# Six of a period's graph products ahead of its first transposes, two in each later slot

## The chip, the core and the metric

The kernel runs on one core of a Trainium2 chip. A core has five engines that work through their own instruction queues and wait for each other on semaphores: PE (TensorE, matrix products; its weight loads are shown apart as PEld), DVE (VectorE), ACT (ScalarE), POOL (GpSimd) and SP (SyncE, which here only starts transfers). The metric is the device time of one execution in microseconds (us), lower is better. Before the change nine runs gave a median of 1305.96 us (1296.56 to 1310.61).

## The reference

Two layers of a graph network over N = 2708 nodes with D = 256 features. Layer 0 multiplies a sparse adjacency by x, projects, applies ReLU, and a layer norm of the sum with x. Layer 1, in which the change lies, is this:

```python
R = S + jnp.eye(N, dtype=X.dtype)
R = R / R.sum(-1, keepdims=True)
...
for n in range(STEPS):
    A = _top_p_attention(Xa, W1, W2, W3)
    Xf = R @ Xf
    Xa = A @ Xa
    Z = Z + Xf @ U1[n].T + Xa @ U2[n].T
h = X + Z
...
return (h - mu) / jnp.sqrt(var + LN_EPS) * ln_g + ln_b
```

STEPS is 2, and a last layer norm of the sum with the layer's input follows. `_top_p_attention` makes N x N probabilities (softmax of q k^T), keeps in each row the largest until their sum reaches 0.9, sets the rest to zero and divides by what is left. R is the sparse graph matrix with its rows divided by their sums.

## The kernel before

Rows are cut into NB = 22 blocks of 128 (the last has 20). Everything is fp32. The order on each engine is the order in which the program calls the instructions (a manual schedule); waits come from the data and from the number of buffers of each tile.

Step 1 of the attention runs in a first loop. Its second step, about 775 us to the end, is a loop over *periods* (`per`, L1336), each of six *slots* (`g`, L1350). It is a pipeline over blocks. In period p:

- PE and ACT make the logits and exponentials of block p+2. The logits come in three parts (L535, tile lg, one buffer of two PSUM banks): part 1 is called in slot 1, part 2 in slot 3, and part 0 of the next block in slot 5. ACT takes the exponentials (`exps2`): two of part 0 in slot 0 (L885, L889), one of part 1 in slot 1, one of part 2 in slot 3 (L885). A part of the logits can only be written when the exponentials of the part before it have been read.
- ACT tries two threshold levels for block p+1 (`try_act`, L1027 and L1030, four passes over 2708 columns in slots 0 to 3, 2.64 us each).
- DVE has a generator of steps (`vector_slots`, L1171): it finishes the levels of block p (L1064 to L1074), masks what is above a level (L1084, slot 1), takes candidates (L1091), and for block p-1 sorts them, finds the threshold, marks ties (L1144, slots 4 and 5) and writes the masked probabilities (L1149, end of slot 5, called *the mask* below).
- PE multiplies the masked block p-2 with ya (`turn` and `products`): in slot g four 128 x 128 transposes into a PSUM tile tr (L562, two buffers), a copy by ACT to wT (L564), and two slots later the four products (L591).

The transposes of slot 0 in a period need the mask that DVE wrote last in the period before.

Into this loop the products with R are put (`r_units`, L775, products at L788). R is stored as a compacted list: for each of the 22 row blocks, CC = 7 chunks of 128 gathered columns and one chunk for its own diagonal block, so 8 products of 128 x 128 by 128 x 256 per row block. There are two passes over the 22 blocks: s = 0 multiplies yf and adds v (results go to v_d), s = 1 multiplies v. `units` (L1316) says how many products a period gets: 12 in period 0, 20 in period 1, 16 (two row blocks) in each of periods 2 to 9 (which end pass 0), none in period 10, 16 in each of periods 11 to 21 (pass 1). What a unit carries with it:

- the first unit of a row block m calls the loads for block m+2: the stored chunks (L755, 448 KB), the diagonal block (L756) and the own rows (L772), all started by SP, and puts seven gathers on a list;
- each unit takes one gather off that list (`y_rows`, L745): an indirect transfer of 128 rows of yf or v into one of three buffers, issued by POOL;
- the last unit of a block loads a base (L800 in pass 0, L811 in pass 1) and puts `r_out` two slots ahead, where DVE scales and adds the sum (L817 or L833, tile misc, two PSUM banks).

Blocks whose two sums have both arrived go into the final norm (`final_slot`, L1282): POOL does two multiply-adds for each of up to two blocks (L1265, L1266, called in slot 0, after ACT's normalisation L1250 of the same slot), DVE takes statistics of the result in slot 4 (L1240, L1241), and the next period's slot 0 normalises and stores them. This begins on POOL with period 13.

The even spread that the change replaces is this:

```python
n = n_r * (g + 1) // NG - n_r * g // NG
```

With n_r = 16 and NG = 6 the slots get 2, 3, 3, 2, 3, 3 products. In slot 0 `r_units(n)` stands ahead of `turn`, in the other slots after it (and ahead of the logits of slot 1).

Of the kernel before, what the change touches and what calls it, by code (L numbers as in the profile page):

```python
# [39 lines left out]
ML = 16  # L40
CW, CC = 128, 7
EARLY = 12
AT = 96


# [17 lines left out]
def gnn_two_layer_kernel(ctx: ExitStack, tc: tile.TileContext, N, xT_d, x_d, adj_d, w0_d, b0_d,  # L63
# [30 lines left out]
    assert SEG * (NS - 1) + 8 <= N <= SEG * NS == SEG2 * NS2 and N >= SEG2 * (NS2 - 1) + 8  # L94
    assert SEG * NS - P == (NB - 1) * P - AT and AT + N - (NB - 1) * P <= P
    assert NB == 3 * KS + 1 and CW == P and CAP % 8 == 0 and N < NB * P
# [63 lines left out]
def fast_path(ctx, tc, c, flags, fint, xT_d, x_d, w0_d, b0_d, w1_d, w2_d, w3_d, u1_d, u2_d, g_d, b_d):  # L160
# [19 lines left out]
    def ps_acc(t=None):  # L180
        acc = ps.tile([P, CH], FP, tag="acc", name="acc")
        if t == NB - 1:
            nc.vector.memset(acc[:, :D + 1], 0.0)
        return acc
# [129 lines left out]
    class Lists:  # L314
# [11 lines left out]
        def turn(self):  # L326
            n = self.n
            parts = names[:, self.a:self.b, :].rearrange("p m (s j) -> p (m s) j", j=3)
            tr = ps_tr()
            for j in range(3):  # L330
                nc.tensor.transpose(tr[:n, j, :], parts[:, :, j], ident)
            nc.scalar.copy(self.row[:n].rearrange("q (j p) -> q j p", j=3), tr[:n, :3, :])
# [136 lines left out]
    lists = Lists(0, ML, flags[:, NF - 4:NF - 2], first_room)  # L469
    order = list(range(EARLY)) + [EDGE] + list(range(EARLY, EDGE))  # L470
    for m, prev, then in zip(order, [None] + order, order[1:] + [None]):
# [37 lines left out]
        if ML <= m < EDGE:  # L509
            i, n = m - ML, EDGE - ML  # L510
# [35 lines left out]
    NG = (NB + 3) // 4  # L546
# [34 lines left out]
    def products(keep):  # L581

        if len(before) > keep:
            p, ks, wT, y, acc = before.pop(0)
            for k in ks:
                if p < P:
                    o = EW * (k % 4)
                    nc.tensor.matmul(acc[o:o + p, :D], lhsT=wT[:, k % 4, :p], rhs=part_y(y, k),
                                     start=k < 4, stop=k >= NB - 4)
                    continue  # L590
                nc.tensor.matmul(acc[:p, :D], lhsT=wT[:, k % 4, :p], rhs=part_y(y, k),  # L591
                                 start=k == 0, stop=k == NB - 1)
# [96 lines left out]
    def ya_pair():  # L689
# [15 lines left out]
        p = rows(t0 + 1)  # L705
        nc.scalar.copy(ya[AT:AT + p, t0 + 1, :], pz[:p, 1, :])

# [67 lines left out]
    def r_units(n):  # L775
        for _ in range(n):
            s, m = r_queue[0]
            p = rows(m)
            if not r_now:
                r_now[:] = [ps_misc() if s or m else ps_acc(), 0]  # L780
                if m + 2 < NB:
                    r_load(s, m + 2, True)
            if to_gather:
                y_rows(*to_gather.pop(0))
            acc, k = r_now
            a, y, own = r_in[s, m]
            kw = CW if k < CC else p
            nc.tensor.matmul(acc[:p, :D], lhsT=a[:kw, k, :p], rhs=y[:kw, k, :] if k < CC else own[:p],  # L788
                             start=k == 0, stop=k == CC)
            r_now[1] += 1  # L790
            if k == CC:
                r_now.clear()
                r_queue.pop(0)
                r_in.pop((s, m))
                base = za_load(m) if s else v_load(m)
                later[1].append(lambda s=s, m=m, acc=acc, base=base: r_out(s, m, acc, base))
# [52 lines left out]
    def e2(t):  # L849
        return ring[t % 5]  # L850
# [30 lines left out]
    def shift(b, lg):  # L881
        nc.vector.tensor_reduce(b.nmax, lg[:, :P], AX.X, ALU.max, negate=True)
# [8 lines left out]
    def begin_search(b):  # L891

        nc.vector.tensor_reduce(b.z, b.all[:b.p, :NL], AX.X, ALU.add)
        yield
        nc.vector.reciprocal(b.rz, b.z)
        nc.vector.tensor_scalar(b.nz, b.z, -1.0, None, op0=ALU.mult)
        yield
        nc.vector.tensor_scalar(b.l0, b.roots, b.roots, b.rz, op0=ALU.mult, op1=ALU.mult)
# [44 lines left out]
    for t in range(NB):  # L943
# [6 lines left out]
        if t == 0:  # L950
            nc.vector.memset(x1_edge, 0.0)
            nc.vector.tensor_copy(x1_edge[AT:AT + rows(EDGE)], x1[:rows(EDGE), EDGE, :])
        for g in range(NG):
# [62 lines left out]
    def fifth():  # L1016
        nonlocal scr
        tile2 = big.tile([P, 2 * NW], FP, tag="V", name="e4")
        ring.append(tile2[:, :NW])
        scr = tile2[:, NW:]  # L1020
# [150 lines left out]
    def vector_slots(a, b, begin):  # L1171


        if b and b.t == 0:
            run_all(in_order(b))
            yield
            run_all(threshold(b))
            yield
            for i in range(WS):
                mark(b, i)  # L1180
            yield
            mask(b)
            yield
            run_all(last_level(a))
            below_level(a)
            yield
            run_all(candidates(a))
            run_all(begin)
            yield
            return  # L1190
        order = in_order(b) if b else None
        levels = last_level(a) if a else None
        cands = candidates(a) if a else None
        limits = threshold(b) if b else None
        run_all(turns((part_of_it(order, 7) if b else None, 1), (levels, 1)))
        yield
        if a:
            below_level(a)
        yield
        run_all(turns((order, 1), (part_of_it(cands, 8) if a else None, 2)))  # L1200
        if a and not b:
            run_all(part_of_it(cands, 8))
        yield
        run_all(turns((limits, 1), (cands, 2)))
        yield
        if b:
            mark(b, 0)
            mark(b, 1)
        yield
        if b:  # L1210
            mark(b, 2)
            mark(b, 3)
            mask(b)
        if begin:
            run_all(begin)
        yield
# [119 lines left out]
    for per in range(NB + 2):  # L1336
        if per == 1:
            fifth()
        if per == NB + 1:
            tail.append(True)  # L1340
        n_r = units.get(per, 0)
        b_act = blocks.get(per + 1)
        t_mul = per - 2 if per > 1 else None
        if t_mul is not None:
            accs[t_mul] = ps_acc(t_mul)
        b_exp = None
        if per and per + 2 < NB:
            b_exp = blocks[per + 2] = Block(per + 2)
        vector = vector_slots(blocks.get(per), blocks.get(per - 1), begin_search(b_exp) if b_exp else None)
        for g in range(NG):  # L1350
            n = n_r * (g + 1) // NG - n_r * g // NG
            now = later.pop(0)
            later.append([])
            if g == 0:
                if b_exp:
                    shift(b_exp, lg[0])
                r_units(n)
            if t_mul == EDGE:
                if g == 0:
                    products(0)  # L1360
                    products(0)
                    edge_product(ya, accs[EDGE], e2(EDGE))
            elif t_mul is not None:
                turn(t_mul, g, ya, accs[t_mul], e2(t_mul))
            if b_exp and g == 3:
                lg = logits(1, b_exp.t, 2)
            if g == NG - 1 and 3 < per + 3 < NB:
                lg = logits(1, per + 3, 0)
            if g:
                r_units(n)  # L1370
            if b_exp and g == 1:
                lg = logits(1, b_exp.t, 1)
            if t_mul is not None and t_mul != EDGE:
                products(2)
            if b_exp and g in (0, 1, 3):
                exps2(b_exp, (g + 1) // 2, *lg)
            if b_act:
                for k, part in {0: ((0, 0),), 1: ((0, 1), (0, 2), (0, 3)), 2: ((1, 0),), 3: ((1, 1), (1, 2), (1, 3))}.get(g, ()):
                    try_act(b_act, k, part)
            if per == 0:  # L1380
                ya_pair()
            next(vector)
            if per == 2 and g == 1:
                nc.gpsimd.memset(ring[4][:, N:], 0.0)
            if g == 0:
                final_slot(0)
                if t_mul:
                    t = t_mul - 1
                    base = za_load(t)
                    later[1].append(lambda t=t, base=base: arrive(t, base, accs.pop(t), ras.pop(t)[:rows(t)]))  # L1390
            for f in now:
                f()
            if g and (per < NB + 1 or g < NG - 1):
                final_slot(g)
# [25 lines left out]
    n = len(new) + len(finals)  # L1420
# [384 lines left out]
```

## Time and profile before

| | us |
|---|---|
| median of nine runs | 1305.96 |
| profiled execution, its own time | 1310.5 |
| its span, first to last instruction | 1308.7 |
| PE busy | 1211.5 (93% of the span) |
| DVE busy | 976.0 |
| ACT busy | 733.4 |
| POOL busy | 633.9 |
| mean granted clock of PE | 0.967 |

A row of the timeline gives the start, the duration, the engine, the line, the operation, out<-in tiles, shapes and how many instructions were merged; in brackets how long the engine was idle before it and what released it. An fp32 product shows as two matmul instructions, a transpose as one. PE's ends are modelled, and some records are missing from the trace (around 1040 to 1047 us, for example). A row of the groups ends with the idle time ahead of the group and its main releaser. Periods are told apart by the masks: the one that ends at 909.72 us is the last of period 6, and the products of period 7 begin on PE at 913.47.

### The profile page before, as it was taken

Reading aid. Unit: us, or ns where it says so; the run is one execution under the profiler, and the core shown is the slowest. Engines: PE = TensorE matmul, PEld = TensorE weight load, DVE = VectorE, ACT = ScalarE, POOL = GpSimd, SP = SyncE. Lnnn points to the kernel's source line nnn. Section 1 sums busy time; section 2 is a strip of 40 time slices with the busy share of each in tenths; the row PEclk is TensorE's granted clock in tenths of the full one; section 3 lists DMA queues with packets and bytes.
Section 4 is the critical chain, followed back from the end, with each engine's and each line's share of the span. In section 5 each row is a group of like instructions: output and inputs, shape, how many; then the busy total and the mean of one; then the engine's idle time right before and its main releaser. Section 6 shows DMA issues by size and latency. Waiting matters only on the chain.

```text
span 1308.7 us, 18668 instructions
## 1 busy us (share of the span) xinstructions
PE 1211.5 (93%) x5772; PEld 915.9 (70%) x5772; DVE 976.0 (75%) x3254; ACT 733.4 (56%) x1299; POOL 633.9 (48%) x596
## 2 busy tenths in 40 slices
PE   8999999998899999989996988989998898999885
PEld 6888878843666777767774566767776676777764
DVE  2455564976998888868750387878999878998886
ACT  2010011045555566556562487878989788999822
POOL 1000000014735434777656377767706857888860
PEclk9999999999899999999998898999999998999898
DMA  7465544424122210232233355555525444565441
GB/s 193 163 190 167 170 145 151 160 96 137 47 91 69 71 39 12 89 95 90 84 72 104 119 172 163 176 173 166 169 52 167 150 133 153 164 191 155 146 117 38
DMA packets 104248, 164.92 MB, mean 126 GB/s; under 512 B 20162, under 2 KB 76870, under 8 KB 104138
## 3 DMA queue, kind: packets, MB, share of 16 engines
q1 hardware_dynamic: 77852, 107.57, 25.4%
q0 software_dynamic: 20544, 51.17, 14.1%
q10 hardware_dynamic: 5742, 4.89, 1.3%
q8 instruction: 48, 0.79, 0.3%
q14 instruction: 62, 0.51, 0.1%
HBM read 129.66 MB, written 33.90 MB: 125 GB/s over the span
## 4 chain that ended last, share of the span: by engine, by line
PE 74%; ACT 9%; DVE 8%; issue 3%; POOL 2%; another core or an unknown queue 2%; DMA 1%; ACTq 0%; POOLq 0%; DVEq 0%
PE acc L591 26%; PE acc L274 12%; PE lg L535 9%; PE misc L788 9%; PE tr L562 7%; PE acc L678 2%; PE misc L410 2%; ACT e L1030 2%; PE acc L699 2%; ACT wT L564 2%; PE misc L449 1%; PE misc L727 1%; POOL yg L745 1%; ACT e L885 1%
## 5 line engine op out<-in xcount | busy, mean ns | idle before, releaser
L564 ACT COPY wT<-tr 128x512 f32<-128x512 f32 (+2 forms) x258 | 136.3, 536 | 242.1 <-PE tr L562 153.0
L591 PE MATMUL acc<-x,wT 128*128 128x256 f32 x882 | 224.8, 396 | 17.3 <-ACT wT L564 17.2
L745 POOL DMA_INDIRECT yg<-v_d,ix x154 | 197.6, 1283 | 81.0 <-issue 36.1
L591 PE MATMUL acc<-ya,wT 128*128 128x256 f32 x924 | 229.6, 390 | 4.7 <-issue 4.7
L745 POOL DMA_INDIRECT yg<-yf_d,ix x154 | 183.1, 1189 | 83.9 <-issue 38.9
L591 PEld LDWEIGHTS acc<-x,wT 128*128 128x128 f32 x882 | 163.0, 194 | 79.8 <-ACT wT L564 31.1
L591 PEld LDWEIGHTS acc<-ya,wT 128*128 128x128 f32 x924 | 175.4, 194 | 45.1 <-issue 22.6
L274 PE MATMUL acc<-y,adj_t 128*128 128x257 f32 x924 | 204.4, 379 | 0.0
L274 PEld LDWEIGHTS acc<-y,adj_t 128*128 128x128 f32 x924 | 173.7, 189 | 26.8 <-issue 1.9
L384 POOL DMA_INDIRECT adj_t<-in_adj,ix x154 | 167.3, 1087 | 51.7 <-issue 43.0
L535 PE MATMUL lg<-k,q 64*128 64x512 f32 (+3 forms) x528 | 140.6, 608 | 32.4 <-ACT e L889 14.8
L788 PE MATMUL misc<-yg,adj_t 128*128 128x256 f32 (+1 forms) x602 | 160.4, 395 | 2.0 <-issue 1.1
L562 PE MATMUL tr<-ident,e 128*128 128x128 f32 (+1 forms) x946 | 148.8, 277 | 14.1 <-DVE e L1149 8.4
L562 PEld LDWEIGHTS tr<-ident,e 128*128 128x128 f32 (+1 forms) x946 | 120.8, 145 | 51.1 <-issue 19.1
L788 PEld LDWEIGHTS misc<-yg,adj_t 128*128 128x128 f32 (+1 forms) x602 | 107.1, 192 | 41.6 <-issue 21.2
L351 POOL DMA_DIRECT2D part_d<-e x1 | 0.6, 576 | 272.5 <-DVE e L350 272.5
L1027 ACT ACTIVATE e<-e,st 128x2708 f32<-128x2708 f32 (+1 forms) x43 | 113.6, 2641 | 0.0
L1030 ACT ACTIVATE e<-e,st 128x2708 f32<-128x2708 f32 (+1 forms) x42 | 110.9, 2641 | 0.0
L462 ACT COPY x1T<-tr 128x256 f32<-128x256 f32 (+1 forms) x22 | 8.0, 364 | 174.6 <-PE tr L461 174.6
L597 DVE MAX8 cand<-e 128x8 f32<-128x170 f32 (+1 forms) x352 | 86.8, 319 | 24.1 <-ACT e L542 18.1
L1091 DVE MAX8 cand<-w 128x8 f32<-128x170 f32 (+1 forms) x352 | 94.1, 321 | 0.1
L535 PEld LDWEIGHTS lg<-k,q 64*128 64x128 f32 (+1 forms) x528 | 40.0, 185 | 65.3 <-issue 23.5
(254 smaller groups left out, 1795.4 us busy)
## 6 DMA issues: line engine op xcount, KB each, us to landing
adj_t<-in_adj SPq DMA_DIRECT2D x42, 704.0 KB
adj_t<-adjc_d SPq DMA_DIRECT2D x44, 448.0 KB
adjc_d<-adj_t SPq DMA_DIRECT2D x22, 256.0 KB
base<-za_d SPq DMA_DIRECT2D x40, 128.0 KB
adjc_d<-adj_t SPq DMA_DIRECT2D x22, 192.0 KB
xt<-in_x ACTq DMA_DIRECT2D x21, 128.0 KB
x_d<-x SPq DMA_DIRECT2D x21, 128.0 KB
x1b_d<-xb SPq DMA_DIRECT2D x21, 128.0 KB
```

The lines of the kernel that those rows point to most:

```text
L274: nc.tensor.matmul(acc[:p, :n], lhsT=halves[k // KH][:, k % KH, :p], rhs=y[:, k, :n], start=k == 0, stop=stop and k == NB - 1)
L384: nc.gpsimd.indirect_dma_start(out=a[:CW, i, :], out_offset=None, in_=adj_rows, in_offset=bass.IndirectOffsetOnAxis(ap=ix[:CW, m, i:i + 1] ...
L535: nc.tensor.matmul(lg[:p, h, at:at + b - a], lhsT=q[o, t * P:t * P + p], rhs=keys[s][o, i, :b - a], start=True, stop=True)
L562: nc.tensor.transpose(tr[:, k % 4, :p], columns(e[:p], k), ident[:p, :p])
L564: nc.scalar.copy(wT[:, :len(ks), :p], tr[:, :len(ks), :p])
L591: nc.tensor.matmul(acc[:p, :D], lhsT=wT[:, k % 4, :p], rhs=part_y(y, k), start=k == 0, stop=k == NB - 1)
L597: nc.vector.max(dst[:p, i * 8:(i + 1) * 8], src[:p, i * step:i * step + w])
L745: nc.gpsimd.indirect_dma_start(out=yg[:CW, m % 3, i, :], out_offset=None, in_=rows_d, in_offset=bass.IndirectOffsetOnAxis(ap=ix[:CW, m, i: ...
L788: nc.tensor.matmul(acc[:p, :D], lhsT=a[:kw, k, :p], rhs=y[:kw, k, :] if k < CC else own[:p], start=k == 0, stop=k == CC)
L1027: nc.scalar.activation(scr[:b.p, :N], e, AF.Relu, bias=b.nz, scale=b.l[k], accum_out=b.relu)
L1030: nc.scalar.activation(scr[:b.p, :N], e, AF.Sign, bias=b.nz, scale=b.l[k], accum_out=b.sign)
L1091: nc.vector.max(b.cand[:p, 8 * i:8 * i + 8], low[:p, SEG2 * i:SEG2 * (i + 1)])
```

## The change

In periods after the first that have products, slot 0 gets six of them and each later slot an equal share of the rest:

```diff
@@ -40,6 +40,7 @@
 ML = 16
 CW, CC = 128, 7
 EARLY = 12
+HEAD = 6
 AT = 96
 
 
@@ -1349,6 +1350,9 @@
         vector = vector_slots(blocks.get(per), blocks.get(per - 1), begin_search(b_exp) if b_exp else None)
         for g in range(NG):
             n = n_r * (g + 1) // NG - n_r * g // NG
+            if per > 1 and n_r:
+                ahead = min(n_r, HEAD)
+                n = (n_r - ahead) * g // (NG - 1) - (n_r - ahead) * (g - 1) // (NG - 1) if g else ahead
             now = later.pop(0)
             later.append([])
             if g == 0:
```

With 16 products the slots get 6, 2, 2, 2, 2, 2. The number of instructions on every engine stays. With the products move their gathers on POOL (six ahead of a period's multiply-adds instead of two), the loads of a period's second row block (from slot 3 to slot 2), and the first row block's base load (slot 2 to 1) and `r_out` (slot 4 to 3, on DVE ahead of the marks).

## The prediction

> **What bounds the kernel now.** The change touches step 2 alone, so I read the page's totals and costliest groups first, then a table of stretches, then the timeline inside single periods.
>
> ```profile
> PE 1211.5 (93%) x5772; PEld 915.9 (70%) x5772; DVE 976.0 (75%) x3254; ACT 733.4 (56%) x1299; POOL 633.9 (48%) x596
> ...
> L535 PE MATMUL lg<-k,q 64*128 64x512 f32 (+3 forms) x528 | 140.6, 608 | 32.4 <-ACT e L889 14.8
> L788 PE MATMUL misc<-yg,adj_t 128*128 128x256 f32 (+1 forms) x602 | 160.4, 395 | 2.0 <-issue 1.1
> ...
> L562 PE MATMUL tr<-ident,e 128*128 128x128 f32 (+1 forms) x946 | 148.8, 277 | 14.1 <-DVE e L1149 8.4
> ```
>
> The last row is what the change addresses: in the whole program the transposes waited 8.4 us for the mask. The table of stretches (us; busy PE, PEld, DVE, ACT, POOL; clock) says where PE has idle time to fill:
>
> ```profile
> 891.20:958.00 66.80, 66.80 (x331) 52.30 (x330) 58.69 (x195) 59.55 (x96) 44.69 (x37) 1.00 0.57 167
> 1105.70:1175.30 69.60, 67.74 (x331) 52.09 (x331) 67.03 (x222) 65.95 (x111) 58.57 (x49) 1.00 0.56 173
> 1175.30:1246.80 71.50, 65.46 (x316) 52.35 (x315) 61.46 (x225) 62.99 (x108) 59.27 (x53) 0.95 0.49 152
> ```
>
> Each row is three periods. In the first (periods 6 to 8) PE is never idle: 22.3 us a period. In the second (15 to 17) a period takes 23.2, in the third (18 to 20) 23.8. One slot 0 and 1 of the first kind, period 7, in the timeline:
>
> ```profile
> 914.34 0.60 PE L562 MATMUL tr<-ident,e 128*128 128x128 f32 x4
> ...
> 914.97 0.59 ACT L564 COPY wT<-tr 128x512 f32<-128x512 f32 x1 [2.16 <-PE misc L788]
> ...
> 916.88 1.11 ACT L889 ACTIVATE e<-lg,st 128x1024 f32<-128x1024 f32 x1
> ...
> 916.94 1.46 PE L788 MATMUL misc<-yg,adj_t 128*128 128x256 f32 x6
> ...
> 918.33 1.13 PE L535 MATMUL lg<-k,q 64*128 64x512 f32 x4
> ```
>
> ACT sat idle 2.16 us until the transposes came, copied them, did two exponentials, and only then the slot's logits could overwrite lg. From transposes to logits it is 3.99 us here, and the same in periods 6 (892.05 to 896.05), 8 (936.62 to 940.61) and 9 (958.90 to 962.89): ACT's chain sets it, and PE's own work fills it to within 0.1. Late in the step the releaser is another:
>
> ```profile
> 1191.86 0.75 POOL L1265 TENSOR_TENSOR u<-u,gb 128x256 f32<-128x256 f32 x1
> 1192.68 0.72 POOL L1266 TENSOR_TENSOR u<-u,x1b 128x256 f32<-128x256 f32 x1
> ...
> 1193.44 0.43 DVE L1240 BATCH_NORM_STATS2 bst<-u 128x6 f32<-128x256 f32 x1 [2.14 <-issue]
> ...
> 1194.93 0.43 DVE L1240 BATCH_NORM_STATS2 bst<-u 128x6 f32<-128x256 f32 x1 [0.85 <-POOL u L1266]
> ...
> 1197.26 3.05 DVE L1149 SCALAR_TENSOR_TENSOR e<-w,st,e 128x2720 f32<-128x2720 f32 x1
> 1197.59 3.54 POOL L745 DMA_INDIRECT yg<-v_d,ix  x1 [0.30 <-issue]
> ...
> 1200.47 0.63 PE L562 MATMUL tr<-ident,e 128*128 128x128 f32 x4 [1.03 <-DVE e L1149]
> ```
>
> POOL's multiply-add ends, DVE's statistics start at once, then the marks, the mask, and the transposes. POOL itself runs without a break from 1089.3 to 1268.3: its groups of multiply-adds start at 1166.20, 1191.86 and 1217.52, 25.7 apart, which is 12 gathers of 0.95+0.30, two that run beside a wide DVE operation (3.54+0.30), and four operations of 0.73 to 0.75 with their spaces. So from period 18 on the mask is late because POOL is full, and PE's wait is only the end of that.
>
> **The change part by part.** No instruction is added or removed on any queue. In 19 periods (2 to 9 and 11 to 21) four of sixteen products move to the front: slots 1 to 5 lose 1, 1, 0, 1, 1.
>
> *Products on PE.* Three products take 1.30 (from 928.23 to the next group at 929.53), so one is 0.43 and four are 1.73. In a PE-bound period the first transposes come 1.73 later, and ACT, which waits for them, with them. Between transposes and slot 1's logits there are now two products instead of three, so PE gets there 0.43 earlier while ACT still needs 3.99: 0.43 of new idle time. Everything else of the 1.73 is work done earlier. Periods 2 to 9: 8 x 0.43 = 3.5. Period 11 had 0.44 of waiting ahead of its transposes which the products now fill: 0. Periods 12 and 13: 0.9. Together +4.3. Bounds: 0, if ACT's start does not follow the transposes, and +13 (second rival).
>
> *The first transposes of period 14.* They start at 1077.54, when the two products end and 0.16 after the mask (1077.38). Four products later they delay ACT's normalisation (L1250), for which POOL's second group waited: 2.27 us, until 1089.33. From that point POOL has no gap, so what is late there stays: +1.7. Bounds 0 and 1.73.
>
> *Gathers on POOL.* Six of a period's gathers instead of two now stand ahead of its multiply-adds: four times 1.25 = 5.0, or 7.6 if one falls under a wide DVE operation. This is paid once, not per period, since 14 gathers still lie between two groups; in periods 2 to 9 there are no multiply-adds and POOL has time (44.7 busy of 66.8). In this execution POOL waited 8.75 and 2.27 for ACT before its first two groups, so the gathers lie in that idle time: 0. Without it the groups come with the gathers' own start (3.5 later) plus 5.0 = 8.5 in place of the 4.3 + 1.7 = 6.0 above.
>
> *Tail.* After period 20's group 8 gathers are left instead of 12, so period 21's comes 5.0 earlier. DVE's wait of 0.84 on it and PE's 0.70 and 0.99 on the last gathers go. Next late is the mask, since DVE is busy 21.0 of that period's 22.35: -0.8. Bounds 0 and -3.4 (PE's waits and its four products, too).
>
> *What costs nothing.* Moved with the products: SP's three loads for the second product (0.32 to 0.43 each, slot 3 to 2; they are needed a period later), the base load (slot 2 to 1, used two slots on as before), and the first product's r_out, 0.48 of DVE, from slot 4 to 3, ahead of the marks. A new meeting: the second product needs the bank that the previous r_out frees in slot 1. In period 7 that ends at 917.71 and PE would come at 922.0; in period 19 (1207.08 against 1206.9) it is 0.2, where PE has idle time anyway. DVE's waits for the previous block's sum in slot 2 (11.0 us in seven waits) grow by up to 1.7; the mask in period 7 was ready 4.6 before its transposes, in 15 to 17 between 3.6 and 1.5, and the transposes move 1.7 too. Were this cover gone, each would cost up to 1.7.
>
> In periods 15 to 17 the same chain on ACT (23.2 busy of 24.2) reaches to slot 5's logits, three products leave it, and a period grows by up to 1.3, to 24.5. That stays under POOL's 25.7, and the 2.14+0.85 that DVE waits in each of periods 18 to 20 absorb it: 0.
>
> Nor do the products shorten the 3.65 and 3.71 us before the masks of periods 20 and 21. They come out of the same period's end, and PE reaches the wait earlier by as much.
>
> Sum: 4.3 + 1.7 - 0.8 = +5.2, or 8.5 - 0.8 = +7.7 where POOL has no idle time to lend. Its 11.0 us are more than 5.0, but the profiled execution took 1310.5 (span 1308.7), 4.5 above the median 1305.96, and idle time of that kind is a likely part of the 4.5. I take +6.0, nearer the first: 1316.5 for the profiled execution, **1312.0** for the median.
>
> *A rule beside the rows.* Around 1084.5 to 1092.0, after the 3.58 us wait for logits at 1081.6, the granted clock was 0.54; it was 0.65 from 872.1 to 877.0, after the 2.72 us wait at 869.4, which is 4.9 x 0.35 x 2 = 3.4 us at half. The Trainium skill (TensorE: Matmul & The Clock Gate, Part 1: The HAM clock gate) states that PE falls to half clock after an idle window of about 3.4 us. The 2.72 us row is shorter than that. By the page a wait of 3.9 or 3.6 cut by 1.3 would keep the clock and save some 3.4 twice, an estimate, which would take the sum from +6 to about -1; by the row 2.7 is enough to lose it, and the sum stays.
>
> **The rivals.**
>
> *1. Faster: the products fill the long waits for logits.* PE waited 14.8 us for L889 in seven waits; 3.91 (period 2), 2.72 (5) and 3.58 (14) are over 2.5, each with a half-clock stretch beside it (6.8, 3.4 and 6.8 us by the granted clock). If ACT's start there hangs on something other than the transposes, three products more run inside each wait (3 x 1.3), and the clock is kept (half of 17.0 = 8.5): -12.4, with what is left of my own terms (+4) about -8: 1298. Against it: before these waits ACT itself sat idle 4.65, 4.25 and 3.73, and PE released it each time. It decides if those copies start when they did, with the transposes 1.7 later.
>
> *2. Slower still: slot 5's logits become ACT's, too.* They need slot 3's exponential, which ended 16.2 after the first copy in period 7 (914.97 to 931.16, 0.59 of it idle). PE would now come 15.9 after its transposes instead of 16.8. Where ACT is later, three products leave the chain and a period costs 1.3: 10 x 1.3 + 1.7 - 0.8 = +13.9, at most 1320; I put it at 1319.
>
> *3. It makes no difference.* The wait of 0.43 is covered in both halves, since ACT takes lost time back from its idle 1.2 to 3.7 a period: 1305. The four equal 3.99 speak against it.
>
> **How the numbers follow.** No change that is under 0.5% (6.5 us) can be told from none here. My sum: 0.52, spread from +4 to +9, of which 0.28 lies beyond 6.5 and 0.24 within. Rival 1: 0.22, faster. Rival 2: 0.22, slower. Rival 3: 0.04, same. So faster 0.22, same 0.28, slower 0.50. Cutting rivals 1 and 2 at their middles leaves 0.2 outside: 1299 to 1320; my own case alone 1310 to 1315.
>
> **What the profile after would show.** Right: first transposes 1.7 later after a period's start; still 3.99 from there to slot 1's logits, with PE idle some 0.4 ahead of them, waiting for L889; periods 6 to 8 at 22.7 instead of 22.3; six gathers ahead of each POOL group, the groups still 25.7 apart and the last gap in gathers gone. Wrong: periods 6 to 8 at 22.3 or less (rival 3 or 1), at 23.5 (rival 2); the waits over 2.5 gone (1); POOL idle between groups after 1090, so that PE's and ACT's longer periods would show in full.

## The result, and the profile after

The changed kernel takes 1314.24 us (median of 20 runs, 1304.67 to 1325.4), the kernel before in the same series 1302.97 (62 runs). The ratio of the fast runs, which leaves out one slow run of the changed kernel, is **1.0081**, 95% interval 1.0061 to 1.0101: 10.6 us slower (the two medians are 11.3 apart), where 6.0 were forecast. Two profiled executions alone would hide this: that of after took 1306.7, 7.6 below its median, that of before 1310.5, 7.5 above. So I compare periods, and of them those that repeat from run to run. The third column is a second profile of the changed kernel, taken with the experiments (masks end to masks end, us):

| periods | before | after | after, again |
|---|---|---|---|
| 2 to 4 | 83.4 | 85.9 | 85.3 |
| 5 | 27.3 | 23.5 | 24.0 |
| 6 to 8 | 67.7 | 70.4 | 70.4 |
| 9 to 11 | 65.8 | 65.0 | 65.0 |
| 12 and 13 | 57.2 | 62.4 | 60.9 |
| 14 | 25.6 | 24.7 | 24.4 |
| 15 to 17 | 71.6 | 73.3 | 73.2 |
| 18 to 20 | 76.7 | 73.6 | 73.3 |
| 21 to the end | 57.4 | 57.6 | 56.0 |

Lines of `kernel.py` after the change are one higher than before up to the loop: L562 is now L563, L889 is L890. First the page's totals and the rows of the groups that answer to those of before:

```profile
PE 1201.6 (92%) x5772; PEld 906.4 (69%) x5772; DVE 978.4 (75%) x3254; ACT 732.7 (56%) x1299; POOL 625.8 (48%) x596
...
L536 PE MATMUL lg<-k,q 64*128 64x512 f32 (+3 forms) x528 | 140.0, 608 | 40.5 <-ACT e L890 20.3
L789 PE MATMUL misc<-yg,adj_t 128*128 128x256 f32 (+1 forms) x602 | 158.4, 392 | 0.6 <-issue 0.6
L563 PE MATMUL tr<-ident,e 128*128 128x128 f32 (+1 forms) x946 | 148.0, 275 | 11.8 <-issue 7.0
```

PE's wait for the logits grew from 32.4 to 40.5 us, and of that the part behind ACT's second exponential from 14.8 to 20.3. The transposes wait less (14.1 to 11.8), and the mask is no longer what they wait for most. The table of stretches for periods 6 to 8, 15 to 17 and 18 to 20 (us; busy PE, PEld, DVE, ACT, POOL; clock):

```profile
877.78:948.15 70.37, 67.05 (x331) 52.29 (x331) 60.56 (x208) 59.65 (x97) 46.56 (x40) 1.00 0.59 166
1100.26:1173.59 73.33, 68.44 (x332) 51.46 (x331) 69.65 (x236) 66.64 (x115) 58.90 (x55) 1.00 0.56 173
1173.59:1247.20 73.61, 67.62 (x334) 53.36 (x332) 69.81 (x235) 64.95 (x116) 60.06 (x54) 1.00 0.56 166
```

PE's work is what it was. In periods 6 to 8 it now stands idle 3.3 us in three periods, where it stood idle not at all: 23.45 a period instead of 22.3. Slots 0 and 1 of period 7 in the timeline:

```profile
906.42 0.60 PE L563 MATMUL tr<-ident,e 128*128 128x128 f32 x4
...
908.01 0.58 ACT L565 COPY wT<-tr 128x512 f32<-128x512 f32 x1 [3.36 <-PE tr L563]
...
909.02 0.60 PE L789 MATMUL misc<-yg,adj_t 128*128 128x256 f32 x2
...
909.46 0.59 PE L789 MATMUL misc<-adj_t 128*128 128x256 f32 x2
...
909.92 1.11 ACT L890 ACTIVATE e<-lg,st 128x1024 f32<-128x1024 f32 x1
...
911.18 1.13 PE L536 MATMUL lg<-k,q 64*128 64x512 f32 x4 [1.13 <-ACT e L890]
```

The place is the forecast one: two products (909.02 and 909.46), then PE waits 1.13 for ACT's exponential. The size is not. From transposes to logits it is 4.76 us, not 3.99, because ACT's copy begins 1.59 after the transposes began; in the period 7 of before it was 0.63. In periods 5, 6 and 8 the copy begins 1.57, 1.57 and 1.55 after the transposes; in period 9 it is back at 0.64, and PE waits 0.17 there. In the second profile the copy of period 5 is at 0.64, too, and those of periods 6 to 8 are at 1.54 to 1.61.

The other surprise is late in the step, in DVE's and POOL's timeline around a group of multiply-adds (now L1266 and L1267):

```profile
1177.41 3.04 DVE L1085 SCALAR_TENSOR_TENSOR w<-e,st 128x2720 f32<-128x2720 f32 x1
...
1178.48 2.79 POOL L746 DMA_INDIRECT yg<-v_d,ix  x1 [0.31 <-issue]
...
1185.59 0.73 POOL L1266 TENSOR_TENSOR u<-u,gb 128x256 f32<-128x256 f32 x1 [0.56 <-ACT u L1251]
...
1186.40 0.73 POOL L1267 TENSOR_TENSOR u<-u,x1b 128x256 f32<-128x256 f32 x1
```

POOL waits 0.56 for ACT ahead of its group: it is not full any more. Its groups start at 1136.62, 1161.11, 1185.59 and 1209.98, 24.4 to 24.5 apart instead of 25.7, and periods 18 to 20 are 3.1 shorter than before.

### The profile page after: what moved, and what is told of

It reads as the page before. It is cut to its first block, busy times and chain, and to the rows that moved or that the text cites. A ratio compares the mean times of both kernels' runs of the same rounds, so it can differ in the third digit from the quotient of the medians.

```text
span 1304.8 us, 18660 instructions
## 1 busy us (share of the span) xinstructions
PE 1201.6 (92%) x5772; PEld 906.4 (69%) x5772; DVE 978.4 (75%) x3254; ACT 732.7 (56%) x1299; POOL 625.8 (48%) x596
## 3 DMA queue, kind: packets, MB, share of 16 engines
q1 hardware_dynamic: 77852, 107.57, 25.7%
## 4 chain that ended last, share of the span: by engine, by line
PE 69%; ACT 16%; DVE 10%; issue 4%; another core or an unknown queue 1%; DMA 0%; ACTq 0%; DVEq 0%
PE acc L592 22%; PE acc L275 12%; PE lg L536 9%; PE misc L789 8%; PE tr L563 6%; ACT e L886 3%; ACT e L1028 3%; PE acc L679 2%; ACT wT L565 2%; ACT e L1031 2%; PE misc L411 2%; ACT e L890 2%; PE misc L728 1%; PE acc L700 1%; PE misc L450 1%
## 5 line engine op out<-in xcount | busy, mean ns | idle before, releaser
L592 PE MATMUL acc<-x,wT 128*128 128x256 f32 x882 | 221.5, 392 | 17.3 <-ACT wT L565 9.8
L592 PE MATMUL acc<-ya,wT 128*128 128x256 f32 x924 | 225.7, 385 | 6.2 <-issue 6.2
L746 POOL DMA_INDIRECT yg<-v_d,ix x154 | 185.8, 1207 | 85.6 <-PE tr L563 43.2
L592 PEld LDWEIGHTS acc<-ya,wT 128*128 128x128 f32 x924 | 172.2, 191 | 45.3 <-issue 24.0
L536 PE MATMUL lg<-k,q 64*128 64x512 f32 (+3 forms) x528 | 140.0, 608 | 40.5 <-ACT e L890 20.3
L563 PE MATMUL tr<-ident,e 128*128 128x128 f32 (+1 forms) x946 | 148.0, 275 | 11.8 <-issue 7.0
L563 PEld LDWEIGHTS tr<-ident,e 128*128 128x128 f32 (+1 forms) x946 | 118.0, 143 | 49.9 <-issue 21.8
```

What stands on the lines that cost most here:

```text
L536: nc.tensor.matmul(lg[:p, h, at:at + b - a], lhsT=q[o, t * P:t * P + p], rhs=keys[s][o, i, :b - a], start=True, stop=True)
L563: nc.tensor.transpose(tr[:, k % 4, :p], columns(e[:p], k), ident[:p, :p])
L746: nc.gpsimd.indirect_dma_start(out=yg[:CW, m % 3, i, :], out_offset=None, in_=rows_d, in_offset=bass.IndirectOffsetOnAxis(ap=ix[:CW, m, i: ...
```

## The experiments

Two theories stood at the start. **A:** the loss sits in the periods that PE bounds, at slot 1's logits. **B:** it comes from the second half (the longer loop of periods 15 to 17, the clock around 12 to 14, POOL). Twelve kernels were run, in four groups.

One thing has to be known for reading them. Kernels of one group share a chip, and the chips were of two kinds. On chip 9 (first group) and chip 14 (last group) the kernel before takes 1256.4 and 1257.3 us; on chip 0 (second group) and chip 6 (third group) it takes 1304.0 and 1307.5, like the runs of before and after above. I call them the 1256 and the 1304 chips, and compare ratios only against before on the same chip.

### Half of the change at a time, and products without gathers (chip 9)

Products ahead in periods 2 to 9 only:

```diff
-            if per > 1 and n_r:
+            if 1 < per < 10 and n_r:
```

> Six products ahead in periods 2 to 9 only; periods 11 to 21 spread as before. Theory A (the loss sits at slot 1's logits of the periods that TensorE bounds: the trace after shows 23.46 us for each of periods 5 to 8 where 22.3 was the rate before, with 1.1 us of TensorE idle at those logits): about 5 x 1.15 = +5.8 over before, 1308 to 1310, and periods 5 to 8 at 23.4 in the profile. Theory B (the loss comes from the second half: the loop of periods 15 to 17, the clock of 12 to 14, the end): within 1 us of before, 1302 to 1304.

Measured: 1260.2 us, ratio **1.0037** (1.0023 to 1.0050). Products ahead in periods 11 to 21 only:

```diff
-            if per > 1 and n_r:
+            if per > 10 and n_r:
```

> Six products ahead in periods 11 to 21 only; periods 2 to 9 spread as before. Theory A: the rest of the change's +10.5, that is about +3 to +5 (periods 15 to 17 each 0.5 longer, period 12 by 1.1, and 18 to 21 some 4 us shorter in all): 1303 to 1308, periods 6 to 8 back at 22.3. Theory B: nearly all of the +10.5, 1311 to 1314.

Measured: 1259.3, **1.0029** (1.0017 to 1.0041). Next, the products of the changed kernel, but POOL's gathers in the slots of before (2, 3, 3, 2, 3, 3). PE's order is that of the changed kernel.

```diff
+    def gathers(n):
+        for _ in range(min(n, len(to_gather))):
+            y_rows(*to_gather.pop(0))
...
-            if to_gather:
+            if gather and to_gather:
                 y_rows(*to_gather.pop(0))
...
+            ng, apart = n, per > 1 and n_r > 0
...
-                r_units(n)
+                r_units(n, not apart)
+                if apart:
+                    gathers(ng)
```

> The products stand as in the changed kernel (6,2,2,2,2,2), POOL's gathers are issued in the slots of before (2,3,3,2,3,3). The copy of slot 0 begins 1.57 us after its transposes in periods 4 to 8 of the changed kernel, 0.64 in those of before and in period 9, which has no gathers. If the six gathers in a row are what delays it, the copy is back at 0.64, TensorE's wait at slot 1's logits falls from 1.1 to 0.43 or less and periods 5 to 8 take 22.4 to 22.8: 1308 to 1311. If the gathers have no part, it is the changed kernel again, 23.45 and 1313 to 1315. The groups of periods 18 to 20 should then be 25.7 apart again if it was the gathers that relieved them, which alone would cost about 4 us.

Measured: 1256.9, **1.0004** (0.9995 to 1.0013). And the reverse, products as before and only the gathers moved (slot 1 finds one and slot 2 none on the list):

```diff
-            if per > 1 and n_r:
-                ahead = min(n_r, HEAD)
-                n = (n_r - ahead) * g // (NG - 1) - (n_r - ahead) * (g - 1) // (NG - 1) if g else ahead
+            ng, apart = (HEAD, 2, 1, 2, 2, 3)[g], per > 1 and n_r > 0
```

> The products stand as before (2,3,3,2,3,3); only POOL's gathers move, six of them to slot 0 and 1,0,2,2,3 to the others. If the gathers' place is what relieved POOL's groups in periods 18 to 21 (94.7 us after, 99.1 before) and costs nothing else: 1298 to 1300. If it was the products' place that did that: 1302 to 1304. If six gathers in a row delay the copy of slot 0 by 0.9, TensorE waits about 0.75 at slot 1's logits in periods 4 to 8 even with three products between: +4, 1306 to 1308.

Measured: 1260.9, **1.0039** (1.0025 to 1.0052).

The early half cost 4.7 us, near the 5.8 of theory A, but not where theory A put them: periods 6 to 8 took 22.5, not 23.45. Three periods each, the stretch from period 6 on and 3.4 us inside period 2, in the run with the early half changed:

```profile
847.15:914.67 67.52, 67.01 (x331) 52.26 (x331) 60.70 (x208) 59.62 (x97) 47.84 (x39) 1.00 0.60 171
...
765.70:769.10 3.40, 3.40 (x12) 2.04 (x9) 3.26 (x19) 3.40 (x4) 2.72 (x4) 0.50 0.74 249
```

and in the run with the late half changed, whose first half is that of before:

```profile
842.01:908.85 66.84, 66.84 (x332) 52.33 (x330) 61.08 (x208) 59.65 (x97) 54.04 (x43) 1.00 0.60 175
...
765.70:769.10 3.40, 3.40 (x19) 2.50 (x18) 3.26 (x14) 3.40 (x4) 2.71 (x3) 1.00 0.81 245
```

The steady price on this chip is 0.2 to 0.25 us a period (67.5 against 66.8 for three). Of the 4.7 us by which periods 2 to 9 are longer (194.7 against 190.0), 3.5 lie in periods 2 to 4. There PE's wait at slot 1's logits of period 2 grew from 1.47 to 1.90, which is one product, and a stretch of 3.4 us at half clock followed in the one run and not in the other. That stretch holds up some 1.7 us of work, an estimate (half of 3.4), which is about half of the 3.5. A later run with the same products ahead and the same 1.90 (the next to last below) had no such stretch, and its periods 2 to 4 are 1.85 shorter; but its loads and gathers stand elsewhere, and an earlier stretch in period 2 was shorter there, too (3.4 us against 6.8). So the share of the clock is not shown by it. Slots 0 and 1 of period 6 in the run with the early half changed show why the steady price is small:

```profile
852.27 0.60 PE L563 MATMUL tr<-ident,e 128*128 128x128 f32 x4
...
852.91 0.59 ACT L565 COPY wT<-tr 128x512 f32<-128x512 f32 x1 [2.41 <-PE tr L563]
...
854.82 1.11 ACT L890 ACTIVATE e<-lg,st 128x1024 f32<-128x1024 f32 x1
...
856.07 1.13 PE L536 MATMUL lg<-k,q 64*128 64x512 f32 x4 [0.17 <-ACT e L890]
```

The copy begins 0.64 after the transposes, and the way from transposes to logits is 3.80. PE's order in these periods is instruction for instruction that of the changed kernel, so the copy that comes at 1.57 elsewhere belongs to the chip as much as to the order.

The second half is a matter of POOL. Periods 15 to 17 and 18 to 20, gathers spread (first fence) and only gathers moved (second):

```profile
1051.93:1124.78 72.85, 67.93 (x329) 51.03 (x328) 69.67 (x235) 66.19 (x113) 60.32 (x54) 1.00 0.57 172
1124.78:1198.14 73.36, 68.71 (x334) 53.15 (x332) 69.97 (x235) 65.00 (x116) 60.52 (x55) 1.00 0.56 169
```

```profile
1047.25:1124.24 76.99, 69.68 (x330) 53.14 (x330) 66.82 (x235) 66.77 (x114) 64.15 (x55) 0.98 0.54 166
1124.24:1200.93 76.69, 66.02 (x314) 52.69 (x314) 66.55 (x234) 62.41 (x105) 63.85 (x55) 0.95 0.51 157
```

With the gathers moved, the groups are 25.6 to 25.7 apart from the first on, and periods 14 to 19 take 25.65 each; the late half of before (read in the run with the early half changed) gets there only in period 16 (23.97, 23.17, 25.66 in periods 14 to 16). With products ahead and gathers spread it never gets there: 24.0 to 24.5 in periods 14 to 20. POOL's busy time differs with it, 64 against 60 in three periods, though the instructions are the same. The 14 gathers between two groups take 18.5 us in the one case and 17.2 to 17.3 in the other, and the difference is in the two that meet a wide DVE operation. In the run with the gathers moved these two take 3.5 to 3.6 each. In the changed kernel above the gather that starts 1.07 after the DVE operation takes 2.79 and ends at 1181.27, 0.82 after the operation's end. In before, as the prediction shows, one that starts 0.33 after it takes 3.54 and ends at 1201.13, again 0.82 after the operation's end. So the price of such a gather is what is left of the DVE operation when it starts, and 0.82 more, and a POOL that is full keeps meeting it early (0.30 to 0.33 into it in six cycles in a row of the run with the gathers moved).

So on this chip the four runs give: early half +0.37%, by products; late half +0.29%, by gathers; products alone +0.04%, a loss in the first half and an equal gain in the second. The stretches agree. Periods 2 to 9 take 190.0 us with the spread of before, 194.7 with products and gathers ahead, 194.9 with products alone and 188.7 with gathers alone. From period 10 to the end it is 322.7 with the spread of before, 326.2 with both ahead, 318.7 with products alone and 328.6 with gathers alone.

### The changed kernel on a 1304 chip, and three variants (chip 0)

The changed kernel itself:

> The changed kernel as it stands, for a profile and a ratio beside the other runs of this call. The first four experiments ran on a chip where before takes 1256.4 and where the periods with six products ahead show 22.5 us, not the 23.45 of the first trace after. If the parts found there add up (early half +0.37%, late half +0.29%), the ratio is 1.0066 with periods 5 to 8 at 22.5 and POOL's groups 25.65 apart in periods 15 to 20; if the copy that begins 1.57 us after slot 0's transposes belongs to the kernel, periods 5 to 8 take 23.4 again and the ratio is 1.008 or more.

Measured: 1312.7, **1.0088** (1.0060 to 1.0116); periods 6 to 8 at 23.4 to 23.5, the copy at 1.54 to 1.61, POOL's groups 24.5 apart. The late copy repeats on this kind of chip. Products ahead only from period 11 on, gathers as before everywhere (with `gathers` as above):

```diff
-            if per > 1 and n_r:
+            ng, apart = n, per > 1 and n_r > 0
+            if per > 10 and n_r:
```

> Products six ahead in periods 11 to 21 only, POOL's gathers everywhere in the slots of before, periods 2 to 9 untouched. Theory A (gathers in slot 0 delay POOL's groups, products ahead do not): periods 15 to 20 at 24.0 to 24.5 as in the run with products ahead and gathers spread, about 4.1 us less than with before's late half, ratio 0.9965 to 0.998. Theory B (that run came out even for another reason): ratio 1.000 to 1.004.

Measured: 1307.1, **1.0032** (1.0004 to 1.0060): theory B's range, although periods 15 to 20 are at 24.2 to 24.5 as theory A wanted. What is gained there must be lost elsewhere, and the profile has one candidate: periods 12 and 13 take 59.3, against 57.2 in before, with 10.2 us at half clock (from 1040.0) where before has 6.8. The same with the gathers of periods 2 to 9 moved ahead:

```diff
-            ng, apart = n, per > 1 and n_r > 0
+            ng, apart = (HEAD, 2, 1, 2, 2, 3)[g] if per < 10 else n, per > 1 and n_r > 0
```

> As the kernel before it in this call, and POOL's gathers of periods 2 to 9 also six in slot 0, 1,0,2,2,3 in the others. Theory A (where POOL has no groups to write, the place of the gathers is free): the same ratio within 0.1%. Theory B (six gathers in a row delay the copy of slot 0 or a product): periods 4 to 8 longer than 22.3 by 0.2 to 0.75 each, +1 to +4 us.

Measured: 1305.4, **1.0006** (0.9982 to 1.0031). Not slower than the one before it, and the copy is at 0.64 to 0.69 in periods 5 to 9. Six gathers in a row do not delay the copy. From period 10 on this kernel and the one before it are the same, so 0.32% and 0.06%, whose intervals overlap, also show how well a chip of this kind tells such differences. Six products ahead in periods 2 to 9 with a third product restored in slot 1, gathers with their products:

```diff
-            if per > 1 and n_r:
-                ahead = min(n_r, HEAD)
-                n = (n_r - ahead) * g // (NG - 1) - (n_r - ahead) * (g - 1) // (NG - 1) if g else ahead
+            if 1 < per < 10 and n_r:
+                n = (HEAD, 3, 1, 2, 2, 2)[g]
```

> Six products ahead in periods 2 to 9, and three again between the first transposes and slot 1's logits (6,3,1,2,2,2), periods 11 to 21 as before. Theory A (the early half loses by the third product that no longer stands before slot 1's logits): TensorE's wait there goes (0.17 per period at 22.5, 1.90 to 1.47 in period 2), periods 5 to 9 at 22.3, the half clock after period 2 does not come, ratio 1.000 to 1.001. Theory B (it is the six ahead of the transposes that lose): periods 5 to 9 stay at 22.5, ratio 1.002 to 1.004.

Measured: 1312.5, **1.0081** (1.0042 to 1.0119). Theory A as I had put it fell on this chip: with three products between, the copy still begins 1.55 and 1.52 after the transposes in periods 5 and 6, PE still waits 0.65 and 0.63 at slot 1's logits, and another 0.36 at those of slot 5, where the changed kernel waits not at all. In periods 7 and 8 the copy is at 0.86 and 0.92 and the period 22.8.

### Products without gathers on a 1304 chip, and the second half alone (chip 6)

Six products ahead in periods 2 to 9, gathers as before:

```diff
-            if per > 1 and n_r:
+            ng, apart = n, per > 1 and n_r > 0
+            if 1 < per < 10 and n_r:
```

> Six products ahead in periods 2 to 9 only, POOL's gathers everywhere in the slots of before, periods 11 to 21 as before. If six gathers in a row are what delays the copy of slot 0 on the chips where before takes about 1304, that copy begins 0.64 us after its transposes, periods 5 to 8 take 22.5 and the ratio is 1.001 to 1.002. If the products alone do it, periods 5 to 8 take 23.4 there and the ratio is 1.004 to 1.008. On a chip where before takes about 1256 the copy is at 0.64 either way, and the run repeats the early half of the run with all products ahead and gathers spread: 1.003 to 1.004.

Measured: 1318.0, **1.0081** (1.0055 to 1.0106), as much as the whole change costs. Period 7 of that run, where L894 is the exponential called L890 above:

```profile
916.64 0.60 PE L563 MATMUL tr<-ident,e 128*128 128x128 f32 x4
...
918.18 0.59 ACT L565 COPY wT<-tr 128x512 f32<-128x512 f32 x1 [3.31 <-issue]
...
921.35 1.13 PE L536 MATMUL lg<-k,q 64*128 64x512 f32 x4 [1.07 <-ACT e L894]
```

The copy begins 1.54 after the transposes without six gathers in a row, and so it does in periods 6 and 8 (1.57 and 1.55); in period 5 it is at 0.64. On a 1304 chip the late copy of these periods comes with the products. Products ahead only from period 14 on:

```diff
-            if per > 1 and n_r:
+            ng, apart = n, per > 1 and n_r > 0
+            if per > 13 and n_r:
```

> Six products ahead only from period 14 on, POOL's gathers everywhere in the slots of before. Theory A (the change gains about 4 us where POOL's groups bound the periods, 18 to 21, and loses it again before period 14): periods 15 to 20 at 24.0 to 24.5, ratio 0.9965 to 0.998, faster than before and than the changed kernel. Theory B (the gain in single profiles comes from the phase in which period 13 ends and not from the products' place): POOL's groups 25.65 apart from period 17 or 18 on, ratio 1.000.

Measured: 1303.5, **0.9953** (0.9919 to 0.9988): by the ratio 6 us faster than before on the same chip (1.6 to 10.6), and the best version of this study. Periods 15 to 17 and 18 to 20:

```profile
1103.91:1177.29 73.38, 68.44 (x331) 51.45 (x331) 69.70 (x235) 66.64 (x115) 58.92 (x55) 1.00 0.57 172
1177.29:1250.88 73.59, 68.38 (x334) 53.06 (x332) 69.83 (x235) 64.91 (x116) 60.08 (x54) 1.00 0.55 166
```

These are the stretches of the changed kernel's first profile to within 0.1 us. The run ahead of it, on the same chip and with the late half of before, takes 71.6 and 76.8 for them. So the gain of 3.1 us in periods 18 to 20 is the change's own, and 1.8 of it are lost again in periods 15 to 17. From the mask of period 13 to the end the single profiles show 229.7 against 231.3; the rest of the 6 us is not seen in them.

### Two last runs on the early half (chip 14, again a 1256 chip)

The kernel with six products ahead in periods 2 to 9 and gathers spread, and with the loads of the row block that begins in slot 0 called in slot 1. The gathers of these periods move to slots 1 to 5, too:

```diff
+                    if gather is None:
+                        held_loads.append((s, m + 2))
+                    else:
+                        r_load(s, m + 2, True)
...
+                while held_loads:
+                    r_load(*held_loads.pop(), True)
+                r_units(n, not apart)
+                if apart:
+                    gathers((0, 5, 3, 2, 2, 2)[g] if 1 < per < 10 else ng)
```

> As the run with six products ahead in periods 2 to 9 and gathers spread (ratio 1.0081, copy of slot 0 at 1.55 us in periods 6 to 8), but the loads of the unit that begins in slot 0 (its adjacency blocks, own rows, and its gathers) are issued in slot 1, after the first transposes, instead of 4.1 us ahead of them. If the landing of these loads beside the transposes is what delays the copy, it begins at 0.64, periods 5 to 8 take 22.5 and the ratio falls to 1.002 to 1.005. If it has no part, the copy stays at 1.5 and the ratio at 1.006 to 1.010. On a chip where before takes about 1256 the copy is at 0.64 anyway, and this tells nothing of it.

Measured: 1262.0, **1.0043** (1.0029 to 1.0056), the copy at 0.64 in periods 4 to 10. On this kind of chip the run can tell nothing of the late copy, as its expectation says. Four products ahead and three in slot 1, gathers with their products:

```diff
+            if 1 < per < 10 and n_r:
+                n = (4, 3, 3, 2, 2, 2)[g]
```

> Four products ahead and three in slot 1 (4,3,3,2,2,2) in periods 2 to 9 only, the rest as before. If the price grows with the number ahead of the transposes, about half of the early half's: ratio 1.003 to 1.005, periods 5 to 8 at 22.6 to 23.0. If only the third product before slot 1's logits matters: ratio 1.000 with periods 5 to 8 at 22.3. If any step beyond two sets the copy back by the 0.95 us: 22.9 to 23.4 and 1.006 or more.

Measured: 1258.3, **1.0012** (1.0003 to 1.0022). Periods 6 to 8:

```profile
844.22:911.07 66.85, 66.85 (x332) 52.32 (x330) 60.88 (x209) 59.66 (x97) 54.06 (x43) 1.00 0.61 174
```

PE has no idle time at all, a period is 22.28, and the wait in period 2 is 1.47 as with the spread of before. Where the copy is on time, the third product ahead of slot 1's logits is the whole of the steady price, and it does not matter that four products stand ahead of the transposes. Of the 0.12% that are left (1.5 us), periods 2 to 4 can hold 1.4: they take 80.0 here and 78.6 with the spread of before on chip 9.

## Why the prediction was right, and where it was not

The direction and the range held, and of the places the new wait at slot 1's logits; the forecast of +6.0 was 4.6 short. The forecast median of 1312.0 lies only 2.2 below the measured one because before's own median came out 3.0 lower in the second series. That the total fell into the range is luck in part: on the 1304 chips the early half cost three times its term, and a gain of 3.1 us that no term had made up for some of it. Two of the signs that the prediction had named as speaking against it appeared: periods 6 to 8 at 23.5, and POOL idle between its groups after 1090. By its own steps:

- **The new wait at slot 1's logits, "8 x 0.43 = 3.5": the mechanism is right, the term is mis-sized, more than any other.** What it measured depends on the chip. On a 1256 chip, and in period 9 on a 1304 chip, ACT's chain is 3.80 and not the 3.99 that I read: in before PE's three products were the later by 0.2, and I took their time for ACT's. So the wait is 0.17 and the period 0.2 to 0.25 longer, not 0.43; only in period 2, where ACT was the later already, it is 0.43 (1.47 to 1.90). On a 1304 chip the copy comes 0.9 later in periods 6 to 8 with six products ahead (in one of three profiles in period 5, too), the wait is 1.1 and the period 1.15 longer. The early half as a whole cost 4.7 us on the one (0.37%) and 10.6 on the other (0.81%). Of the 10.6, the three periods account for 3.5; the rest is not located. My upper bound of +13 contained that, the value I took did not.
- **The start of the step, periods 2 to 4:** I had put only 0.43 a period there. On the 1256 chip it was 3.5 in three periods, of which the half clock after the longer wait was some 1.7 by the estimate above. On the 1304 chips single runs of periods 2 to 4 scatter from 82.6 to 92.9, and the share of the change in it can't be read.
- **Period 14's transposes, +1.7:** not seen. POOL's second group starts 12.05 after the mask of period 13 (12.34 in the second profile), in before 11.95.
- **Gathers ahead of POOL's groups, 0 or +2.5:** the condition was right. On the 1304 chips POOL had the idle time and they cost nothing there. On the 1256 chip they make POOL the bound of periods 14 and 15, too, and cost 0.39%, some 5 us, when they move alone.
- **Periods 15 to 17 "up to 1.3, to 24.5":** right to the tenth, 24.4 to 24.5, with the waits of PE on the logits of slots 1, 3 and 5 and the transposes (0.17, 0.45, 0.36, 0.65). That they would be absorbed was not right: the three periods take 1.7 more in all (71.6 to 73.3).
- **"The groups still 25.7 apart", so that 18 to 20 stay as they are:** wrong, by a gain. I took the two gathers of 3.54 for a constant. They are what is left of a DVE operation; in the changed kernel they take 2.59 and 2.80, and POOL's cycle without its wait of 0.53 to 0.57 is 24.0, below the 24.5 of ACT's loop. Here 3.1 us came back that no term had. (The 23.8 a period that the prediction read for 18 to 20 in before leaves out the 3.71 us ahead of period 21's transposes; by the masks it was 25.6.)
- **The tail, -0.8:** period 21 is 1.25 shorter (22.35 to 21.10) in both profiles of the changed kernel, 22.2 to 22.9 where products are ahead and the gathers spread. Right, within its bounds.
- **Periods 12 and 13, 0.9:** longer in the four profiles with six products ahead from period 11 on a 1304 chip (58.8 to 62.4, against 57.2 in before and 52.4 to 57.3 in the three others). All four have 10.2 us at half clock there, before and the three others 3.4 to 6.8. Leaving periods 11 to 13 alone turned +0.32% and +0.06%, from two kernels with the same second half, into -0.47%, on different chips of the same kind. That the clock is the cause is argued, not shown.

Of the rivals, the second had the right size for the wrong place: 23.45 where it said 23.5, but slot 5's logits do not wait in periods 5 to 8; all of the idle time is at slot 1's. The first fell by the time, which went up, but what it named is not refuted. In the first profile after, the transposes of periods 2 and 14 come 2.1 and 1.2 later after the mask than in before, yet ACT's copies start at the same time after it (19.53 and 4.76, in before 19.47 and 4.66), and the waits shrank from 3.91 and 3.58 to 2.27 and 2.93. So there the copies seem to hang on something other than the start of the transposes. In the second profile the two waits are 4.14 and 0.17, so single profiles can't price it. The rival's rows, waits of 3.91, 2.72 and 3.58 in before, belong to the 1304 chips: on chip 9 the same half of the program waits 1.47 in period 2 and not at all in period 5. The rule on the clock was rightly left out of the sum as a gain, but as a loss it was missed: half clock came after a wait of 1.90 in two runs.

What delays the copy on the 1304 chips stays open. The trace records the semaphore event that releases it 1.53 to 1.57 after the transposes' start in the late periods and 0.61 in the others, while PE's next events come on time in both. The Trainium skill (Perfetto Trace Analysis, Tensor Engine Instruction) states that a matmul's reported start is the start of its data fetch, that its end is estimated, and that the semaphore is pushed only when PSUM has acknowledged the writes; so the rows of PE can't show it. Late copies are not the change's alone: in before, too, the copies of periods 2, 5 and 14 begin 3.09, 3.78 and 4.50 after their transposes, while on the 1256 chips none of slot 0 in periods 4 to 18 begins more than 0.70 after. And six products ahead do not always bring them: in periods 15 to 19 of the changed kernel the copy is at 0.64. Gathers in a row are not the cause (with products as before: 0.64), nor is the missing third product alone (with it: 1.55 and 1.52 in periods 5 and 6, 0.86 and 0.92 in periods 7 and 8). Landing loads alone are not, either. Around the transposes of period 7 (906.42, copy late) and of period 16 (1128.69, copy at 0.64) of the changed kernel the DMA engines are about equally busy (the last two numbers: their share, GB/s):

```profile
904.00:909.00 5.00, 5.00 (x28) 4.38 (x28) 5.00 (x16) 1.64 (x4) 4.09 (x4) 1.00 0.76 257
1126.00:1131.00 5.00, 5.00 (x28) 4.36 (x27) 4.79 (x17) 2.99 (x10) 4.08 (x4) 1.00 0.81 281
```

Whether the loads have a part was to be tried by moving them, but that run met a 1256 chip.

## What to carry to other kernels

A way that is the same four times need not be set by the engine you think of: when two chains end within 0.2 us of each other, subtract each from the rows before pricing a change to one. A transfer or operation that is stretched by another engine is no constant; its price is what is left of the other when it starts, and a saturated queue can leave that state as soon as something shifts the phase. And a reordering that helps one stage of a pipeline and hurts another should be made by stage: here the same six products ahead cost 0.81% in one half and, with the gathers left in their places, gain 0.47% (0.12% to 0.81%) from period 14 on.

## What was not expected of the hardware

- **Chips of one type differ.** The same program takes 1256 us on two chips and 1303 to 1307 on the others, and on the former the runs of before in one group lie within 5 us, on the latter within 18. In the first step DVE ends its wide operation (L662 in before, e<-e,th) 22 times; from the fifteenth to the twenty-first these ends lie 16.35 to 17.45 us apart on the former and 15.45 to 20.82 on the latter, and the first mask of step 2 ends at 768 to 779 instead of 741 to 744. A measured ratio is then one of a chip: six products ahead in periods 2 to 9 cost 0.37% to 0.43% on the one kind and 0.81% on the other.
- **Half clock after short waits.** On chip 9 a stretch of 3.4 us at half clock followed a wait of 1.90 us in two runs, as one followed 2.72 in before; on chip 14 the same 1.90 was not followed by one, nor were waits of 2.26 and 2.94 late in the run with the early half changed. The Trainium skill (TensorE: Matmul & The Clock Gate, Part 1: The HAM clock gate) states an idle window of about 3.4 us; these waits are shorter, and here the measurement decides.
- **A gather on POOL that meets a wide two-input DVE operation ends 0.82 after it**, whether it started 0.33 or 1.07 into it (3.54 and 2.79 long). One that started before the operation (1177.23, against 1177.41) took its usual 0.95. The Trainium skill (SBUF — State Buffer, SBUF: two separate sides) states that whichever of the two starts first holds the shared port and the other is blocked. The trace agrees where the DVE operation starts first; where the gather does, the DVE operation is no longer for it (3.04, where 3.03 to 3.05 is usual).
